# A two-layer graph network on one core: gates as diagonal products in nine blocks, another step count at the end, and gathers issued in twos

## The chip, the core and the metric

The kernel runs on one core of a Trainium2 chip. A core has five engines that work side by side, each on its own queue of instructions in order: PE (matrix products, with weight loads shown apart as PEld), DVE (vector work), ACT (activations, scaled copies), POOL (here: the indirect gathers) and SP (here: it issues the plain DMA transfers). They wait for one another through semaphores. The metric is device time in microseconds for one execution; each version is timed in several runs and the median is compared.

## What is computed

Four layers, each added onto the node values `x` (6250 nodes of 256 numbers), after a layer norm. The middle two halves matter most here:

```python
# layer 0, graph: 106250 edges sorted by dst
h = relu(concat([x[src], edge_attr]) @ W1 + b1)
agg = segment_sum(h, dst) / max(count, 1)
x = x + relu(concat([x, agg]) @ W2 + b2)
# layer 0, attention picks 2 of 4 experts by node
e = leaky_relu(a_src[src] + a_dst[dst])          # 131072 edges and own loops
agg = segment_sum(h[src] * softmax_over_dst(e))
gate = softmax(top2(mean_heads(layernorm(agg))))
x = x + sum_e gate[:, e] * (gelu(x @ W1[e] + b1[e]) @ W2[e] + b2[e])
# layer 1, graph
h = relu(x @ Wp.T + bp)
agg = sqrt(segment_sum(edge_weight * (h ** 2)[src], dst))
x = x + h @ W1.T + b1 + agg @ W2.T + b2
# layer 1, experts: a shared three-layer net and 4 small experts, 2 chosen by a gate
```

## The kernel before

Nodes lie in 49 blocks of 128, the node values stay in `x_all` on the chip. The work has four stages.

**First layer** (L1369 to L1545). Edges are handled 6 columns of 128 at a time; a group is three pairs of columns. For each pair `turn` transposes the edge features, `hidden` multiplies them (`ph`, L1091), adds the gathered source rows (L1417, DVE) and applies relu (L1422, ACT); `add_up` sums over destinations with 0/1 matrices (L1443). `load_sources` issues the six gathers of a group on POOL into a tile `yg` with three buffers; in the first groups a POOL copy into a small tile `seen` (L1386) stands in front of them.

**Attention, with the first expert layer woven in** (L1552 to L2142). The loop over `k` is called a tick here: 80 groups of 8 edge columns plus 5 ticks to finish. In a tick, `fetch` issues 8 gathers into `sg` (5 buffers), `score` and `weigh` work on earlier groups, `spread_out` and `add_up` sum into `acc`. `slot` is called four or five times a tick; it advances the experts by one step (`first` writes the hidden tile `hh` on ACT, L1607; `second` multiplies on), runs steps of `node_values`, and loads finished expert outputs.

**The seam.** When the sums of a range of blocks are done, `gates` computes their gates and `node_values` adds the gated expert outputs onto `x_all`: four multiply-adds on DVE for each block (L1952). Then come norm, transposes, the projection, and the write of `hp` to memory (L1996). The ranges end at 8, 16, 24, 32, 36, 40, 44 and 49 blocks. The gathers of the last stage read `hp_dram` and wait for all 49 writes.

**Last layer** (L2145 to L2473). 139 groups of six gathers on POOL (`hg`, six buffers, four groups ahead); `weights_of` builds weighted 0/1 matrices on DVE (L2390); `add_up` sums them on PE (L2411). Nodes are in 16 blocks of 4, 2 or 1. When a block is complete, `roots` adds the bias `b12` onto its node values (L2422) and takes the square root; `end_of2` finishes a node block, `gates2` and `experts2` are its expert layer. These are generators: `step_ends` advances all `end_of2` by a step, `advance(routes, 1)` the gates, `advance(layers, n)` the experts by n steps. In a group's turn up to group 103 it is one step of ends, one of routes and three of layers; from group 104 (`LATE`) two, two and four.

The order on each engine is not the order of the program text: the framework that builds the program lists instructions by its own estimate of when each is ready, so work of a later stage can stand on an engine in front of the end of an earlier one. The helpers `mm` (L1091), `transposed` (L1085) and `gather` (L1104) record all their instructions under one line each.

Of the kernel before, what the change touches and what calls it, by code (L numbers as in the profile page):

```python
# [841 lines left out]
def kernel(ctx: ExitStack, tc: tile.TileContext, a: dict, out: bass.AP):  # L842
# [74 lines left out]
    with ExitStack() as fast:  # L917
# [362 lines left out]
        with ExitStack() as layer:  # L1280
# [81 lines left out]
            with (  # L1362
# [9 lines left out]
                seen = wy.tile([P, 1], F32, name="seen")  # L1372
# [9 lines left out]
                def load_sources(q):  # L1382

                    if 1 <= q <= 3:
                        p, j = (q - 2, G1 - 1) if q > 1 else (0, 0)
                        GP.tensor_copy(seen, hbuf[p % 2][:, j, 0:1])  # L1386
                    w, g = groups1[q]
                    sources[q] = wk.tile([P, G1, D], F32, name="yg", bufs=3)
                    for j, (k, t) in enumerate(chunk(g)):
                        gather(sources[q][:, j, :], y_dram, src1[:, w, k, t : t + 1])  # L1390
# [16 lines left out]
                def hidden(k):  # L1407
                    q, j = pairs[k]
                    ph = psh.tile([P, 2, D], F32, name="ph")
                    e = et.pop(k)  # L1410
                    for i in range(2):
                        mm(
                            ph[:, i, :], lambda c: e[:, i, c * P : (c + 1) * P],
                            lambda c: w1b[:, c, :],
                        )
                    y = sources[q][:, j : j + 2, :]
                    V.tensor_add(y, ph, y)  # L1417
                    h = hbuf[q % 2]
                    if j == 0:

                        SC.activation(h[:, :, D:WS], ones[:, 0:G1].unsqueeze(2), AF.Copy)
                    SC.activation(h[:, j : j + 2, 0:D], y, AF.Relu)  # L1422
# [95 lines left out]
                load_sources(0)  # L1518
# [3 lines left out]
                load_sources(1)  # L1522
                for k in range(len(pairs)):
                    if k + 3 < len(pairs):
                        turn(k + 3)
                    if k + 1 < len(pairs):
                        hidden(k + 1)

                    q = k // NPC
                    if k % NPC == 0 and q:  # L1530
                        add_up(q - 1)
                    if k == len(pairs) - 1:
                        add_up(q)
                    if k % NPC == 1 and q + 2 < len(groups1):
                        load_sources(q + 2)
                    for n in list(work):
                        if next(n, work) is work:
                            work.remove(n)
                    if k % (NPC * NG) == 0 and k:
                        work.append(end_of(k // (NPC * NG) - 1))  # L1540
                    if k == len(pairs) - 1:
                        work.append(end_of(T - 1))
# [28 lines left out]
        def experts1():  # L1571
# [24 lines left out]
            def first(u, f0):  # L1596
# [9 lines left out]
                for f in (f0, f0 + 1):  # L1606
                    SC.activation(  # L1607
                        hidden[u][:, f, :n, :], ph[:, f - f0, :n, :], AF.Gelu,
                        bias=b1[:, e, f : f + 1],
                    )  # L1610

# [42 lines left out]

        layers = [experts1()]
        part = sums.tile([P, 3, T, H], BF16, name="part")
        with (
# [33 lines left out]
            def fetch(g):  # L1691
                got[g] = wk.tile([P, G, GW], F32, name="sg", bufs=5)
                for j in range(G):
                    gather(got[g][:, j, :], gat_dram, src2[:, g * G + j : g * G + j + 1])
# [250 lines left out]
            def node_values(ws):  # L1945
# [4 lines left out]
                for i, w in enumerate(ws):  # L1950
                    for e in range(X):
                        V.scalar_tensor_tensor(  # L1952
                            x_all[:, w, :], ys.pop((w, e)), gate[:, w, e : e + 1], x_all[:, w, :],
                            op0=OP.mult, op1=OP.add,
                        )
# [150 lines left out]
            for k in range(NA + 5):  # L2106
                if k < NA:
                    fetch(k)
# [5 lines left out]
                slot()  # L2114
                if now in range(NA):
                    score(now, 0)
                slot()
                if here in range(NA):
# [5 lines left out]
                slot()  # L2124
                if 0 <= before < NA:
                    add_up(before, 1)
                slot()
                if now in range(NA):
# [28 lines left out]
        with (  # L2157
# [62 lines left out]
            def end_of2(b, i, root):  # L2220
# [8 lines left out]
                V.tensor_add(x_all[:, w, :], x_all[:, w, :], pm)  # L2229
                st = wk.tile([P, 6], F32, name="ln_st")  # L2230
# [188 lines left out]
            def roots(b):  # L2419
                n = blocks[b][1]  # L2420
                at = slice(blocks[b][0], blocks[b][0] + n)
                V.tensor_add(  # L2422
                    x_all[:, at, :], x_all[:, at, :],
                    b12[:, None, :].to_broadcast([P, n, D]),
                )
# [23 lines left out]
            LATE = len(groups2) * 3 // 4  # L2449
# [6 lines left out]
            while k < len(groups2) or complete or coming or ends or routes or layers:  # L2456
# [6 lines left out]
                advance(layers, 1)  # L2463
                step_ends(k)
                if k >= LATE:
                    advance(layers, 1)
                    advance(routes, 1)
                while complete:
                    coming += roots(complete.pop(0))
                advance(routes, 1)  # L2470
                advance(layers, 2)
                if k >= LATE:
                    step_ends(k)  # L2473
# [72 lines left out]
```

## Time and profile before

| | us |
|---|---|
| runs | 3552.38, 3555.01, 3555.68 |
| median | 3555.01 |
| profiled execution | 3555.79 |
| its span, first to last instruction | 3554.0 |

Mean granted PE clock over the span: 0.911 of full speed. Where the stages lie in the profiled execution:

| from to, us | what |
|---|---|
| 0 to 132 | norms and first products, edge windows |
| 132 to 1425 | first layer |
| 1429 to 2424 | attention and first experts (first gather of sg to last sum of acc) |
| 2424 to 2468 | the seam |
| 2468 to 3506 | last layer, from the first to the last gather of hg |
| 3506 to 3554 | its tail |

How to read the views: the busy table by stretch gives for each engine how long it worked in it and how many instructions ran. A timeline line gives start, duration, engine, line of the kernel, operation, output and inputs with shapes, and in brackets the idle time in front of it and what ended it. A line of waits gives engine, line, what it waited for, then the total, the number of times and the longest.

### The profile page before, as it was taken

What the parts mean: (1) busy time and instruction counts of PE and PEld (TensorE: products, weight loads), DVE (VectorE), ACT (ScalarE), POOL (GpSimd) and SP (SyncE); (2) the same over time, 40 slices, a digit from 0 to 9 for tenths busy, and PEclk for the clock granted to TensorE, in tenths of its full rate; (3) what the DMA queues carried; (4) which work ended last, traced back from release to release, by engine and by line L of the source; (5) the groups of instructions that cost most, each with busy time, mean ns of one, the idle gap of its engine ahead of it and who ended that gap; (6) DMA issues with size and microseconds to landing.
All of it is one profiled execution on the core that took longest, in us unless ns stands there. A gap on an engine that the chain in (4) does not pass through costs nothing.

```text
span 3554.0 us, 57573 instructions
## 1 busy us (share of the span) xinstructions
PE 3338.9 (94%) x20063; PEld 2662.0 (75%) x20063; DVE 2170.1 (61%) x6210; ACT 1412.1 (40%) x2750; POOL 2252.3 (63%) x2367
## 2 busy tenths in 40 slices
PE   7999999999999999999999999997678988989898
PEld 3577777777777778888888888895456666666677
DVE  9999996444544444787758576977234444444464
ACT  4444444444444444444544454664011212211133
POOL 0376666666666664676656555662777777777773
PEclk9999999999999999999999999998567776777797
DMA  6456656656555554433434343553112222222221
GB/s 174 128 189 189 184 183 184 186 186 182 183 183 188 181 183 142 110 97 96 125 88 127 83 130 84 154 94 109 52 53 59 60 59 59 59 59 60 65 62 37
DMA packets 342928, 428.52 MB, mean 121 GB/s; under 512 B 139174, under 2 KB 246453, under 8 KB 342630
## 3 DMA queue, kind: packets, MB, share of 16 engines
q1 hardware_dynamic: 245174, 244.98, 22.1%
q0 software_dynamic: 89408, 178.08, 19.4%
q8 instruction: 162, 2.65, 0.3%
q10 hardware_dynamic: 8048, 1.68, 0.2%
q14 instruction: 136, 1.11, 0.1%
HBM read 382.05 MB, written 42.49 MB: 119 GB/s over the span
## 4 chain that ended last, share of the span: by engine, by line
PE 66%; POOL 14%; DMA 7%; issue 7%; DVE 4%; ACT 1%; SPq 0%; ACTq 0%; POOLq 0%; DVEq 0%
PE ph L1091 32%; POOL hg L1104 13%; PE py L1091 10%; PE pt L1085 7%; PE pe L1443 6%; PE po L1771 5%; DMA hg<-hp_dram,src 5%; PE pt L1091 2%; DMA rb<-low_dram 1%; PE pe L2411 1%; PE pa L1708 1%; PE pm L1091 1%; DVE junk L982 1%; DVE key L1240 0%; DVE order L1237 0%
## 5 line engine op out<-in xcount | busy, mean ns | idle before, releaser
L1104 POOL DMA_INDIRECT yg<-y_dram,src x882 | 847.0, 960 | 543.1 <-issue 226.7
L1104 POOL DMA_INDIRECT hg<-hp_dram,src x831 | 785.7, 946 | 269.2 <-issue 224.3
L1104 POOL DMA_INDIRECT sg<-gat_dram,src x640 | 614.1, 960 | 350.1 <-issue 161.5
L1091 PE MATMUL ph<-w1b,et 128*128 128x256 f32 x3528 | 835.7, 380 | 0.0
L1091 PEld LDWEIGHTS ph<-w1b,et 128*128 128x128 f32 x3528 | 637.0, 190 | 68.7
L2411 PE MATMUL pe<-eq,hg 128*128 128x96 f32 (+15 forms) x2036 | 439.9, 353 | 148.9 <-DMA hg<-hp_dram,src 120.6
L2411 PEld LDWEIGHTS pe<-eq,hg 128*128 128x128 f32 x2036 | 388.2, 260 | 251.8 <-issue 94.6
L1417 DVE TENSOR_TENSOR yg<-ph,yg 128x512 f32<-128x512 f32 x441 | 303.3, 688 | 375.3 <-PE ph L1091 370.7
L2390 DVE TENSOR_SCALAR eq<-px,dst,ew 128x96 f32<-128x96 f32 x831 | 262.0, 370 | 217.2 <-PE pe L2411 120.6
L1091 PE MATMUL ph<-b_all,w 128*128 128x256 f32 (+1 forms) x1600 | 387.1, 380 | 1.5 <-ACT hh L1607 1.4
L1091 PE MATMUL py<-w,hh 128*128 128x256 f32 x1568 | 383.1, 384 | 5.0 <-ACT hh L1607 4.5
L1086 ACT ACTIVATE et<-pt 128x512 f32<-128x512 f32 x441 | 262.2, 596 | 254.4 <-PE pt L1085 242.1
L1422 ACT ACTIVATE h<-yg 128x512 f32<-128x512 f32 x441 | 276.1, 626 | 215.4 <-DVE yg L1417 209.0
L1091 PEld LDWEIGHTS py<-w,hh 128*128 128x128 f32 x1568 | 288.7, 190 | 41.2 <-ACT hh L1607 6.6
L1091 PEld LDWEIGHTS ph<-b_all,w 128*128 128x128 f32 x1600 | 290.0, 190 | 33.7 <-ACT hh L1607 2.0
L1607 ACT ACTIVATE hh<-ph,b 128x256 f32<-128x256 f32 (+1 forms) x400 | 166.7, 467 | 285.6 <-PE ph L1091 279.7
L1085 PE MATMUL pt<-ident,ea 128*128 128x128 f32 x1764 | 272.1, 277 | 3.4 <-ACT et L1086 3.4
L1085 PEld LDWEIGHTS pt<-ident,ea 128*128 128x128 f32 x1764 | 210.2, 144 | 65.0 <-issue 40.4
L1771 PE MATMUL po<-pp,B 128*128 128x240 f32 (+10 forms) x1280 | 252.1, 337 | 2.2 <-DVE acc L1777 2.1
L1771 PEld LDWEIGHTS po<-pp,B 128*128 128x128 f32 x1280 | 215.6, 190 | 14.3 <-DVE acc L1777 2.8
L1443 PE MATMUL pe<-h,eq 128*32 128x257 f32 x3168 | 216.8, 384 | 3.7 <-ACT h L1422 1.9
L1443 PEld LDWEIGHTS pe<-h,eq 128*32 128x32 f32 x3168 | 96.2, 109 | 102.6 <-issue 35.0
(330 smaller groups left out, 4264.5 us busy)
## 6 DMA issues: line engine op xcount, KB each, us to landing
ea<-in_edge_attr_dram SPq DMA_DIRECT2D x147, 768.0 KB
y<-y SPq DMA_DIRECT2D x196, 128.0 KB
w<-in_L_ffn_W_dram SPq DMA_DIRECT2D x48, 512.0 KB
y<-ys SPq DMA_DIRECT2D x96, 256.0 KB
rb<-low_dram SPq DMA_DIRECT2D x80, 256.0 KB
yg<-y_dram,src POOLq DMA_INDIRECT x882
hg<-hp_dram,src POOLq DMA_INDIRECT x831
sg<-gat_dram,src POOLq DMA_INDIRECT x640
```

Of the source, the lines that this page charges most:

```text
L982: V.tensor_scalar(junk, flat, float(w * P), None, op0=OP.is_lt, op1=OP.add, accum_out=below[:, w : w + 1],)
L1085: TE.transpose(pt[:, c, :], src[:, c * P : (c + 1) * P], ident)
L1086: SC.activation(dst, pt.rearrange("p c k -> p (c k)"), AF.Copy)
L1091: TE.matmul(dst, lhs(c), rhs(c), start=c == 0, stop=c == n - 1)
L1104: GP.indirect_dma_start(out=dst, out_offset=None, in_=table[0:NP, :], in_offset=IndirectOffsetOnAxis(ap=idx, axis=0),)
L1417: V.tensor_add(y, ph, y)
L1422: SC.activation(h[:, j : j + 2, 0:D], y, AF.Relu)
L1443: TE.matmul(sums[w][b * Q : (b + 1) * Q, :], eq[k][:, j, at], h[:, i * NT + j, :], start=g == 0 and j == NT - 1, stop=g == last_of[b] and ...
L1607: SC.activation(hidden[u][:, f, :n, :], ph[:, f - f0, :n, :], AF.Gelu, bias=b1[:, e, f : f + 1],)
L1771: TE.matmul(po.rearrange("p b v -> p (b v)"), B[:, j, :], pp[:, j, 0:n, :].rearrange("p b v -> p (b v)"), start=half == 0 and j == 0, stop ...
L2390: V.tensor_scalar(equals[k][:, j, :], lanes[:, 0:NW], dst_of[:, t : t + 1], ew[:, t : t + 1], op0=OP.is_equal, op1=OP.mult,)
L2411: TE.matmul(sums[b][:, lo - t0 * P : hi - t0 * P], hg[:, j, :], eq[:, j, lo - n0 : hi - n0], start=False, stop=after >= (t0 + n) * P,)
```

## The change

Four edits.

1. First layer: `load_sources` takes a pair, not a group. `yg` tiles hold two columns, with nine buffers for three of six columns. For pairs 3 to 8 a POOL copy writes one element of each column of the gather's own tile from a relu output two pairs back, and the gathers follow it. In the loop, one or two pairs are issued per turn, up to six ahead.
2. Attention: `fetch` issues two gathers, and is called four times in a tick, after slots one to four. From the second group on, a POOL copy of the newest expert result (`newest`, set by `first`) into the gathers' tile stands in front of each two.
3. Seam: for blocks 40 to 48 (`LATER = T - 9`) the four multiply-adds become four scaled copies of the identity on ACT (`dg`, one buffer), four products on PE and one add on DVE.
4. Last layer: the bias `b12` is added in `end_of2`, block by block, and no longer in `roots`. A group's turn is a loop over one, two (from `LATE`) or three (from the last twelve groups, `LAST12`) rounds of: layers one step, ends, routes, and layers one more step (two before `LATE`).

```diff
-                def load_sources(q):
-
-                    if 1 <= q <= 3:
-                        p, j = (q - 2, G1 - 1) if q > 1 else (0, 0)
-                        GP.tensor_copy(seen, hbuf[p % 2][:, j, 0:1])
+                def load_sources(k, after):
+
+                    q, j = pairs[k]
                     w, g = groups1[q]
-                    sources[q] = wk.tile([P, G1, D], F32, name="yg", bufs=3)
-                    for j, (k, t) in enumerate(chunk(g)):
-                        gather(sources[q][:, j, :], y_dram, src1[:, w, k, t : t + 1])
+                    sources[k] = wk.tile([P, 2, D], F32, name="yg", bufs=3 * NPC)
+
+                    if NPC <= k < 3 * NPC:
+                        p, i = pairs[after]
+                        h = hbuf[p % 2][:, i, 0:1]
+                        GP.tensor_copy(sources[k][:, :, 0:1], h.unsqueeze(1).to_broadcast([P, 2, 1]))
+                    for i, (n, t) in enumerate(list(chunk(g))[j : j + 2]):
+                        gather(sources[k][:, i, :], y_dram, src1[:, w, n, t : t + 1])
...
+                    for _ in range(2):
+                        if loaded < min(k + 2 * NPC + 1, len(pairs)):
+                            load_sources(loaded, k + 1)
+                            loaded += 1
...
+                newest[0] = hidden[u][:, f0, 0, 0:1]
...
-            def fetch(g):
-                got[g] = wk.tile([P, G, GW], F32, name="sg", bufs=5)
-                for j in range(G):
+            def fetch(g, j0):
+
+                if j0 == 0:
+                    got[g] = wk.tile([P, G, GW], F32, name="sg", bufs=5)
+                if g > 0:
+                    GP.tensor_copy(
+                        got[g][:, j0 : j0 + 2, 0:1],
+                        newest[0].unsqueeze(1).to_broadcast([P, 2, 1]),
+                    )
+                for j in range(j0, j0 + 2):
                     gather(got[g][:, j, :], gat_dram, src2[:, g * G + j : g * G + j + 1])
...
+                    if w < LATER:
+                        for e in range(X):
+                            V.scalar_tensor_tensor(
+                                x_all[:, w, :], ys.pop((w, e)), gate[:, w, e : e + 1],
+                                x_all[:, w, :], op0=OP.mult, op1=OP.add,
+                            )
+                    else:
+
+                        dg = n6.tile([P, X, P], F32, name="dg", bufs=1)
+                        for e in range(X):
+                            SC.activation(dg[:, e, :], ident, AF.Copy, scale=gate[:, w, e : e + 1])
+                        py = psy.tile([P, 2, D], F32, name="py")[:, 0, :]
+                        mm(py, lambda e: dg[:, e, :], lambda e: ys.pop((w, e)), X)
+                        V.tensor_add(x_all[:, w, :], x_all[:, w, :], py)
...
                 V.tensor_add(x_all[:, w, :], x_all[:, w, :], pm)
+                V.tensor_add(x_all[:, w, :], x_all[:, w, :], b12)
...
             def roots(b):
                 n = blocks[b][1]
-                at = slice(blocks[b][0], blocks[b][0] + n)
-                V.tensor_add(
-                    x_all[:, at, :], x_all[:, at, :],
-                    b12[:, None, :].to_broadcast([P, n, D]),
-                )
...
-            LATE = len(groups2) * 3 // 4
+            LATE, LAST12 = len(groups2) * 3 // 4, len(groups2) - 12
...
-                advance(layers, 1)
-                step_ends(k)
-                if k >= LATE:
+                for n in range(1 + (k >= LATE) + (k >= LAST12)):
                     advance(layers, 1)
+                    step_ends(k)
                     advance(routes, 1)
-                while complete:
-                    coming += roots(complete.pop(0))
-                advance(routes, 1)
-                advance(layers, 2)
-                if k >= LATE:
-                    step_ends(k)
+                    if n == 0:
+                        while complete:
+                            coming += roots(complete.pop(0))
+                    advance(layers, 2 if k < LATE else 1)
                 k += 1
```

## The prediction

> **What bounds the kernel now.** I read the page's busy shares and clock first, then the busy time by stretch, then the waits and the instruction sequence at the seams between stages.
>
> ```profile
> PE 3338.9 (94%) x20063; PEld 2662.0 (75%) x20063; DVE 2170.1 (61%) x6210; ACT 1412.1 (40%) x2750; POOL 2252.3 (63%) x2367
> PEclk9999999999999999999999999998567776777797
> ```
>
> PE is busy 94% of the span, but with two meanings: its clock is full in the first 28 slices and about 0.7 after. The next table tells the stages apart (start:end, length, busy PE, PEld, DVE, ACT, POOL, then clock, DMA share, GB/s).
>
> ```profile
> 600.00:800.00 200.00, 200.00 (x1440) 158.68 (x1433) 90.69 (x255) 93.38 (x195) 132.68 (x139) 1.00 0.62 184
> ...
> 1440.00:2424.00 984.00, 975.51 (x6788) 867.38 (x6785) 711.17 (x1745) 499.19 (x871) 605.99 (x632) 1.00 0.41 107
> ...
> 2427.00:2464.00 37.00, 25.18 (x121) 18.56 (x119) 33.68 (x109) 22.87 (x55) 4.07 (x3) 0.91 0.58 176
> ...
> 3474.00:3495.00 21.00, 20.98 (x77) 18.62 (x77) 8.68 (x37) 4.80 (x11) 15.95 (x17) 0.50 0.23 66
> ...
> 3506.00:3544.00 38.00, 35.64 (x209) 27.49 (x207) 26.26 (x124) 23.52 (x58) 0.32 (x1) 1.00 0.06 17
> ```
>
> First layer: PE has no idle time at full clock. Attention: 8.5 us of PE idle in 984. Then a seam, 2427 to 2464, where DVE is busy 33.7 of 37 us: blocks 40 to 48 get their gated sum, norm and projection, and nothing of the next stage may gather before the last projection lands. The last stage runs from the first to the last gather of hg:
>
> ```profile
> 2467.64 0.95 POOL L1104 DMA_INDIRECT hg<-hp_dram,src  x1 [16.20 <-DMA eb<-in_L_ffn_eb_dram]
> ...
> 3505.38 0.94 POOL L1104 DMA_INDIRECT hg<-hp_dram,src  x1 [0.30 <-issue]
> ```
>
> From 2467.64 to 3506.32 is 1038.7 us for 831 gathers, 1.25 us each, 0.94 busy and 0.30 of issue, without a break: POOL's issue sets this stage and the change leaves it alone. After it PE works off a remainder until 3544 and the output leaves. So time can only be won or lost at the edges of the first two stages, in the seam, and in the tail.
>
> **The gathers in twos.** The built order of PE, ACT and DVE is the same as before, buffer names aside, up to the seam; only POOL's changes.
>
> ```profile
> L1386 POOL COPY seen<-h x3: 198/202/203, 144.3 to 163.4; 128x1 f32<-128x1 f32 x3
> ...
> POOL sg L1104 <- DVE px L1743: 128.7, 40, 6.1
> ```
>
> First layer: three copies on POOL become six. In steady state a pair waits for the buffer freed nine pairs earlier, in place of six for a group; the work is the same and PE has no idle time to give. At the start the old copies held back nothing they did not write: nine gathers ran from 132.3 to 144.3 without a stop. The new copies write into the gathers' own tiles, so the seventh gather waits for the second pair's relu, about 141.5, in place of 139.7 (2 us), and whatever is late then is the sum at DVE. PE has ph in three buffers and idled 6.5 us of 50 between 130 and 180. I take +1 us; bounds -3 (half of that idle) and +4 (two pairs' gathers late).
>
> Attention: 316 copies on POOL, four a tick, each 0.20 us by the row above; there the next gather started 1.29 us after the last instead of 1.25, so a copy mostly fits in the issue gap. At worst a tick needs 8 x 1.25 + 4 x 0.2 = 10.8 us of POOL; a tick lasts 968.4 / 79 = 12.3 us (first and last equality of rb, 1437.2 and 2405.6, 80 of them). The copy waits for the newest ACT result, and behind it wait the gathers of its tick, used three ticks (37 us) later. ACT in turn must not overwrite the hidden tile before the copy has read it; it has two buffers and comes back some four expert steps later, 9.7 us (100 units of four steps in 968.4 us). So I cost it at nothing: the 1.5 us a tick that POOL has left over hide it, and if they did not, 80 x 0.8 = 64 us would be exposed. Bounds: -5 (much of the 8.5 us of PE idle) and +6 (a few short ticks in which ACT waits on POOL).
>
> **The seam.** Nine blocks lose four multiply-adds on DVE each and get four ACT copies of the identity scaled by the gate, four matmuls and one add.
>
> ```profile
> L1952 DVE SCALAR_TENSOR_TENSOR x_all<-y,gate,x_all 128x256 f32<-128x256 f32 x196 | 86.1, 474 | 0.7 <-DMA y<-y 0.2
> ...
> L1989 ACT ACTIVATE b_all<-py,bp 128x128 f32<-128x128 f32 x49 | 17.9, 368 | 23.3 <-PE py L1091 23.0
> L1995 ACT ACTIVATE hp<-py 128x128 f32<-128x128 f32 x49 | 13.2, 275 | 25.0 <-PE py L1993 21.5 <-DMA w<-in_L_ffn_W_dram 2.8 <-DMA hp_dram<-hp 0.6
> ...
> 2456.38 1.23 DVE L2422 TENSOR_TENSOR x_all<-x_all,b 128x1024 f32<-128x1024 f32 x1
> 2457.53 0.15 DVE L1965 RECIPROCAL ln_rs<-ln_rs 128x1 f32<-128x1 f32 x1
> 2457.60 1.21 DVE L2422 TENSOR_TENSOR x_all<-x_all,b 128x1024 f32<-128x1024 f32 x1
> 2458.72 0.15 DVE L1966 SCALAR_TENSOR_TENSOR off<-ln_mv,ln_rs 128x1 f32<-128x1 f32 x1
> ```
>
> DVE: 15.8 us of multiply-adds go (36 in this stretch), 9 x 0.42 come (an add of that shape), and the two bias adds of L2422 that stand between the last block's reciprocal and offset go as well (2.4): 33.7 - 15.8 + 3.8 - 2.4 = 19.3 us. DVE is no longer the limit. ACT: 36 scaled copies, between 0.25 (the spacing of back-to-back 128x128 activations, two in 0.61) and 0.37 (L1989, which also reads a per-partition operand), 9.0 to 13.2 us; the built order has seven table loads where the trace has five, 2 x 1.28. 22.9 + 9.0 + 2.6 = 34.5 to 38.7 us. PE: a 128x256 product of four is 1.73 us at full clock, nine of them 15.6; 25.2 + 15.6 = 40.8 us. From that comes about 2 for two 128x512 fills that ran at half clock (3.99 us), and about 4 for expert matmuls (twelve 128x256 products, 24 records, 3.98 us) that the new order puts ahead of the first diagonal product: 34.8. So the stretch of 37 us is exchanged from one engine at 34 for two at 35 to 38 which must hand each block to and fro: the scaled tile has one buffer, so ACT waits for PE at each block and PE for ACT. Bounds: -4 (PE's 34.8 with little idle, and DVE's 2.4 on the last block's chain gone) and +12 (the full ACT sum, 38.7, two thirds of a microsecond of hand-over at each of nine blocks, 6, and half the clock for a quarter of the products, 4). I take +4, PE's sum plus 6 us of hand-overs.
>
> The page "ScalarE: Activation LUTs" (section "What ACT_TABLE_LOAD costs") gives a switch 2.66 us with its drain; the two extra would then be 5.3 us and the seam +7. The rows do not show the drain: the load at 3503.79 takes 1.28 and its activation starts at 3505.08.
>
> **The tail.** In both orders I count the matmuls of this path behind the last one that uses a gather: 86 before, 59 after; one whole single-node block (46) moves in front of it. Before, these take from 3513.0 to 3544.0 on a PE that is 94% busy: 31.0 / 86 = 0.36 us each, so 27 fewer are 9.7 us. Against it: the bias add becomes one more 0.42 us add in each block's chain, two blocks deep in the tail (0.8), and the chain of the last block (norm, transposes, logits) shows more as PE empties. I take -7.5, between -11 (with the 4.2 us that the last gather's matmul was behind its landing, 3508.75, partly won) and -2. For the moved 9.7 us must fit before: from 3415 to 3506 PE is busy 88.5 of 91 us at clock 0.83, so only 2.5 us are free unless the clock rises; the stretch 3474 to 3495 above, busy throughout at 0.50, is where it would have to. The other 47 bias adds (20 us over 1000, for 15 us of wide ones) lie on a DVE busy under half of the last stage; if it were full they would cost 5.
>
> The page "TensorE: Matmul & The Clock Gate" (section "Part 1: The HAM clock gate") says the clock comes back after about 3.4 us of steady work. The row speaks against it: 21 us busy without a gap at 0.50. By the rule the moved work fits and the tail gains 10; by the row it runs at half speed and the gain is nearer the small bound.
>
> **Sum.** +1 + 0 + 4 - 7.5 = -2.5 us. The profiled execution took 3555.8 us (span 3554.0 and 1.8 around it), 0.8 above the median of the three runs; I apply the sum to the median: 3552.5.
>
> **The rivals.** About 0.2%, 7.1 us, is what a measurement of this kernel can tell from no change.
> - Forecast, 0.40: the seam gives back most of what the tail wins, 3552.5, own range 3548 to 3562.
> - The seam opens, 0.35: ACT and PE overlap block by block, and the end of DVE's queue is what held the projections. Seam -4, tail -10, start and attention -2: 3539. For it: DVE at 33.7 of 37, and the bias adds in front of the last block's offset. Against it: PE's new sum.
> - The single-buffered diagonal takes DVE's place, 0.25: at each block ACT writes (1.0 to 1.5 us), PE multiplies (1.73), and the next pair's transposes wait in PE's queue behind it; seam +12, tail -3, start +1: 3565. With the tail at -3 it decides from where the hand-overs exceed 11 us in the nine blocks (34.8 + 11 - 37 = +9, and the sum above +7). For it: the buffer. Against it: the built order puts other work of ACT and PE between the four copies of a block.
> - The twos do nothing, whichever of these holds: PE has 15 us of idle time in all of both stages' 130 to 180 and 1440 to 2424, which is also the most they could win.
>
> Independent errors of about 8 (seam), 4.5 (tail), 5.5 (attention) and 3.5 (start) combine to 11 us; widened for the outer cases the range is 3535 to 3568. Faster 0.35, same 0.40, slower 0.25.
>
> **What would show it.** Seam: the first gather of hg near 2472; DVE under 25 us busy between the last gates and it, ACT or PE above 33. Tail: last gather to last matmul near 30 us, from 37.7. Attention: L1743's wait on POOL replaced by waits on hh, PE idle still under 12 us. It is wrong if PE idles more than 15 us in the attention, if the hg gathers no longer come every 1.25 us, or if the seam ends earlier than 2464.

## The result, and the profile after

| | before | after |
|---|---|---|
| median, us (runs) | 3555.35 (4) | 3577.05 (4) |
| lowest to highest | 3552.38 to 3559.82 | 3575.96 to 3579.52 |
| ratio | | 1.0061, 95% interval 1.0049 to 1.0073 |
| span of the profiled execution | 3554.0 | 3574.1 |
| granted clock of PE, mean | 0.911 | 0.919 |

The change makes the kernel 0.6% slower, about 22 us. The prediction was 3552.5 with a range of 3535 to 3568, so the time lies 9 us above the range and 12 above the slower rival.

In the runs e5 to e8 and e9 to e12 below, each set taken together, every kernel took over 4250 us, the unchanged one too (medians 4359.74 and 4357.78), for a reason that is not known, so these runs are compared only within their set.

The page of the kernel after: busy time by engine, and the granted clock in 40 slices.

```profile
PE 3332.0 (93%) x20135; PEld 2646.8 (74%) x20135; DVE 2166.2 (61%) x6216; ACT 1426.6 (40%) x2788; POOL 2316.5 (65%) x2686
PEclk9999999999999999999999999998557877877798
```

The totals hardly move: PE 7 us less, POOL 64 us more (the copies). The stretches tell more. Busy time by stretch of the kernel after (start:end, length, PE, PEld, DVE, ACT, POOL, clock, DMA share, GB/s); the second is the seam, from the gates of blocks 40 to 43 to the last square of hp:

```profile
1440.00:2424.00 984.00, 972.08 (x6759) 862.80 (x6758) 709.94 (x1736) 496.18 (x866) 672.44 (x949) 1.00 0.43 107
2430.96:2480.53 49.57, 40.97 (x195) 31.49 (x195) 18.14 (x75) 36.16 (x93) 4.07 (x3) 0.97 0.48 138
```

The first and the last gather of hg, from POOL's timeline after:

```profile
2482.93 0.95 POOL L1104 DMA_INDIRECT hg<-hp_dram,src  x1 [23.62 <-DVE ew L2228]
...
3522.88 0.95 POOL L1104 DMA_INDIRECT hg<-hp_dram,src  x1 [0.30 <-issue]
```

From such landmarks the 20.1 us between the two spans divide without a rest:

| stretch | before, us | after, us | difference | predicted |
|---|---|---|---|---|
| start to first gather of sg | 1429.44 | 1430.19 | +0.75 | +1 |
| to the last sum of acc | 995.44 | 998.74 | +3.30 | 0 |
| to the first gather of hg (seam) | 42.76 | 54.00 | +11.24 | +4 |
| to the last gather of hg | 1037.74 | 1039.95 | +2.21 | 0 |
| to the end (tail) | 48.62 | 51.22 | +2.60 | -7.5 |

Two terms are wrong by 7 and by 10 us; the experiments are about these. The other three differences are no larger than what the profiles differ by anyway. In the profiles of the experiments below that took the usual time, the first gather of sg comes at 1426.4 to 1429.8 us where edit 1 is absent, the attention takes 993.5 to 997.4 us where edit 2 is absent, and the gathers of hg take 1036.1 to 1039.1 us.

### The profile page after: what moved, and what is told of

Its sections match the earlier page's. It is cut to its first block, busy times and chain, and to the rows that moved or that the text cites. A ratio compares the mean times of both kernels' runs of the same rounds, so it can differ in the third digit from the quotient of the medians.

```text
span 3574.1 us, 58710 instructions
## 1 busy us (share of the span) xinstructions
PE 3332.0 (93%) x20135; PEld 2646.8 (74%) x20135; DVE 2166.2 (61%) x6216; ACT 1426.6 (40%) x2788; POOL 2316.5 (65%) x2686
## 4 chain that ended last, share of the span: by engine, by line
PE 67%; POOL 12%; issue 7%; DMA 6%; DVE 5%; ACT 1%; SPq 0%; ACTq 0%; POOLq 0%; DVEq 0%
PE ph L1091 32%; POOL hg L1104 11%; PE py L1091 10%; PE pt L1085 7%; PE pe L1445 6%; PE po L1787 5%; DMA hg<-hp_dram,src 3%; PE pt L1091 3%; PE pe L2443 3%; POOL sg L1104 1%; DMA rb<-low_dram 1%; PE pa L1724 1%; DVE junk L982 1%; DVE x_all L1969 0%; DVE key L1240 0%
## 5 line engine op out<-in xcount | busy, mean ns | idle before, releaser
L2443 PE MATMUL pe<-eq,hg 128*128 128x96 f32 (+15 forms) x2036 | 431.7, 347 | 167.3 <-DMA hg<-hp_dram,src 132.3
L2443 PEld LDWEIGHTS pe<-eq,hg 128*128 128x128 f32 x2036 | 372.6, 252 | 272.8 <-issue 103.8
```

Of the source, the lines that this page charges most:

```text
L2443: TE.matmul(sums[b][:, lo - t0 * P : hi - t0 * P], hg[:, j, :], eq[:, j, lo - n0 : hi - n0], start=False, stop=after >= (t0 + n) * P,)
```

## The experiments

"Seam" is the time from the last sum of acc to the first gather of hg, "root" from the last gather of hg to the last square root of a sum, "rest" from there to the last sum of x_all. They come from one profile each; ratios go against the kernel before, run in the same set.

| run | kernel | ratio (95%) | seam | root | rest |
|---|---|---|---|---|---|
| | before | | 42.8 | 7.8 | 31.7 |
| | after | 1.0061 (1.0049 to 1.0073) | 54.0 | 12.2 | 30.5 |
| e1 | edit 1 alone | 1.0002 (0.9993 to 1.0011) | 43.3 | 4.1 | 31.7 |
| e2 | edit 2 alone | 1.0007 (0.9998 to 1.0016) | 43.1 | 6.5 | 31.7 |
| e3 | edit 3 alone | 1.0051 (1.0037 to 1.0064) | 61.7 | 5.4 | 31.7 |
| e4 | edit 4 alone | 1.0012 (1.0003 to 1.0021) | 44.7 | 12.3 | 30.5 |
| e13 | after, next pair early | 1.0048 (1.0032 to 1.0065) | 52.9 | 12.3 | 30.4 |
| e14 | after, three buffers | 1.0065 (1.0048 to 1.0081) | 57.8 | 14.1 | 28.9 |
| e15 | e4, equalities earlier | 1.0032 (1.0022 to 1.0042) | 44.7 | 19.8 | 29.6 |
| e16 | e4, third step stopped | 0.9998 (0.9988 to 1.0007) | 43.7 | 9.2 | 27.2 |
| e17 | before, half the products | 1.0059 (1.0042 to 1.0076) | 52.1 | 6.0 | 42.3 |
| e18 | after without edit 3 | 1.0026 (1.0016 to 1.0035) | 42.9 | 12.3 | 30.5 |

**Each edit by itself (e1 to e4).** The lines of edit 1, 2, 3 or 4 of the diff, put alone into the kernel before.

> The kernel before with the first layer's gathers in twos and nothing else. Theory (each stage's difference between the two traces belongs to the edit in that stage): the first gather of sg starts 0.75 us later, at 1430.2 in place of 1429.4, nothing later changes, and the time is 0 to +2 us against before. Rival (the stages are coupled: a different order on POOL at the start also shifts the attention): the attention's 995.2 us from its first gather to its last sum grows by some of the 3.3 us seen with all parts, and the time is +3 to +5 us.

The first gather of sg came at 1429.01, and the attention took 994.5 us. Neither theory's cost is there: edit 1 alone does nothing that can be measured (the interval of the time is -2.5 to +3.9 us).

> The kernel before with the attention's gathers in twos behind copies, and nothing else. Theory: the stretch from the first gather of sg to the last sum is 998.5 us in place of 995.2, the seam behind it stays 43.0 us (last sum to first gather of hg), and the time is +3 to +4 us against before. Rival (the copies on POOL and the waits of ACT for them are what delays the seam): the seam grows too, by most of the 11 us seen with all parts, and the time is +10 us or more.

Attention 995.7 us and seam 43.1: the rival falls. The 3 to 4 us of the theory are not in this profile either, though the interval of the time (-0.7 to +5.7 us) does not exclude them. With all parts the attention took 998.7, 998.3 (e13) and 1002.6 (e14), with all but the diagonals 997.5 (e18). But e4, which leaves the attention as it was, took 997.4, just under the lowest of these, so whether edit 2 costs anything together with the others is not shown.

> The kernel before with the diagonal products for the last nine blocks, and nothing else. Theory (the diagonals alone open the seam): the attention stays 995.2 us, the seam from the last sum to the first gather of hg is 52 to 55 us in place of 43.0, the tail behind the last gather of hg stays 48.6 us, and the time is +9 to +12 us against before. The wide bias adds still stand in DVE's queue at the end of the seam here, so up to 2.4 us more. Rival (the seam is long only because the attention ends in another order on POOL and ACT): the seam stays within 2 us of 43 and the time within 3 us of before.

The theory's side holds, but the price is higher than it said: a seam of 61.7 us, and a time 17 us over before (medians 3571.73 and 3554.67). DVE's timeline of this kernel shows why it is worse alone than with edit 4:

```profile
2458.62 1.22 DVE L2434 TENSOR_TENSOR x_all<-x_all,b 128x1024 f32<-128x1024 f32 x1
2459.76 0.42 DVE L1969 BATCH_NORM_STATS2 ln_st<-x_all 128x6 f32<-128x256 f32 x1
2460.09 1.21 DVE L2434 TENSOR_TENSOR x_all<-x_all,b 128x1024 f32<-128x1024 f32 x1
...
2464.36 1.19 DVE L2434 TENSOR_TENSOR x_all<-x_all,b 128x1024 f32<-128x1024 f32 x1
2465.47 0.15 DVE L1971 TENSOR_SCALAR ln_rs<-ln_mv 128x1 f32<-128x1 f32 x1
```

The wide bias adds of the next stage, of which two stood in front of the last offset before, now stand one by one between the steps of a norm. PE then waited 6.46 us for that norm's xn. With all four edits the seam is 61.7 - 54.0 = 7.7 us shorter; as edits 1 and 2 leave it alone, this is put down to edit 4, which takes these adds away.

> The kernel before with three steps in the last twelve ticks and the bias added in each node block's own step, and nothing else. Theory (the extra steps stand ahead of the last gathers' products in PE's and DVE's queues, so the last block's root comes 4 us later and gives back what the shorter remainder saves): the stretch behind the last gather of hg is 50 to 52 us in place of 48.6, the seam is 2 to 3 us shorter without the wide adds in DVE's queue, and the time is 0 to +3 us against before. Rival (the tail was long with all parts only because the clock of TensorE fell to 0.59 in one stretch of 10 us): behind the last gather it is 43 us or less here, and the time is 6 to 9 us under before.

The tail is 51.7 us, as the theory had it; the rival's 43 is far off. But the seam did not get shorter without the wide adds (44.7). That is the first sign that it did not wait for these 7 us of DVE's work.

**The seam without the diagonals, and with other makers and buffers (e5 to e8).** Each changes one thing in the kernel after.

```diff
 e5  -  dg = n6.tile([P, X, P], F32, name="dg", bufs=1)
     +  dg = wk.tile([P, HG, P], F32, name="B", bufs=3)
 e6  as e5, and
     -  SC.activation(dg[:, e, :], ident, AF.Copy, scale=gate[:, w, e : e + 1])
     +  GP.tensor_scalar(dg[:, e, :], ident, gate[:, w, e : e + 1], None, op0=OP.mult)
 e7  -  if w < LATER:
     +  if w < LATER or w % 2 == 0:
 e8  -  LATER = T - 9
     +  LATER = T
```

> The changed kernel with the scaled identity in the three buffers of tile B, which the attention has done with by then, in place of one buffer of its own. The stretch from the last sum of the attention to the first gather of hg was 54.0 us in the changed kernel and 42.8 before. Theory (PE's queue makes the pairs serial: the next pair's diagonal products stand behind this pair's transposes, which wait for its norm): only the waits of PE for the scaled identity go, 1.1 us in some of the pairs, so the stretch is 50 to 53 us and the time 1 to 4 us under the changed kernel. Rival (the single buffer is what makes ACT and PE take turns, as the prediction's slower side had it): the stretch falls to 43 to 46 us and the time by 8 to 11 us, to within 0.3 to 0.4% of before.

> As the run with three buffers, and POOL, which is idle in that stretch, writes the scaled identities in place of ACT. Theory (PE's queue): ACT was not what the pairs waited for, so the stretch is within 2 us of the run with three buffers. Rival (ACT's queue is the limit: 36 scaled copies and the table loads between them, 38 us by the prediction's full sum): ACT loses 36 copies of 0.3 us, and the stretch is 6 to 10 us shorter than with three buffers.

> The changed kernel with diagonal products for the odd ones of the last nine blocks only (41, 43, 45, 47), the even ones by DVE as before. Theory (PE's queue): one product of 2.0 us in each pair's chain in place of two and DVE's sum of the other beside it, so four pairs get 1.5 to 2 us shorter each: the stretch is 46 to 49 us in place of 54.0. Rival (DVE's queue is what held the stretch before, so half of its work away must shorten it against before): under 42 us.

> The changed kernel without the diagonal products: the gathers in twos and the three steps stay. Theory (the diagonals cost the seam 10 to 12 us, and the rest of the change costs 5 to 6 in all): the stretch is 43 to 45 us and the time 3 to 7 us over before. Rival (with the steps of the tail the seam is long anyway, because the order of the queues is made anew): the stretch stays over 48 us.

Seams: 57.5 (e5), 57.3 (e6), 50.3 (e7), 43.5 (e8). POOL as maker gives nothing over ACT, though ACT is then busy for 24.2 us of the stretch in place of 36.0, so ACT's 36 copies are not the limit; and three buffers leave the seam 14 us above the one without products, over both the theory's 50 to 53 and the rival's 43 to 46. Half the products do not bring it under 42, as the rival of e7 had it. The ratios against the kernel before are 0.9824 (0.9787 to 0.9860), 0.9840 (0.9793 to 0.9888), 0.9802 (0.9765 to 0.9840) and 0.9800 (0.9763 to 0.9837). They are not taken for a gain, as no run at the usual time shows it. In these eight profiles the attention takes 1235 to 1252 us with the twos and 1312 us without (e12), so edit 2 may have won something here that it does not win otherwise; this was not followed up.

**The same again, and the bias alone (e9 to e12).** e9, e10 and e11 are e5, e7 and e8; e12 is the kernel before with `V.tensor_add(x_all[:, w, :], x_all[:, w, :], b12)` in `end_of2` in place of the wide add in `roots`.

> The same kernel as the first run with three buffers for the scaled identity, again, since in that call every kernel, the one before too, took over 4260 us. Theory (PE's queue makes the pairs serial): from the last sum of the attention to the first gather of hg 50 to 53 us (54.0 in the changed kernel, 42.8 before), and the time 1 to 4 us under the changed kernel, 3573 to 3576. Rival (the single buffer makes ACT and PE take turns): 43 to 46 us, and 3566 to 3569.

> Again, for the same reason: diagonal products for blocks 41, 43, 45 and 47 only. Theory (PE's queue): 46 to 49 us for the stretch in place of 54.0, and 3569 to 3573 us. Rival (DVE's queue is what held the stretch before, so taking half of its work must shorten it against before): under 42 us.

> Again, for the same reason: the changed kernel without the diagonal products. Theory (the diagonals cost this stretch 10 to 12 us and the rest of the change 5 to 6 in all): 43 to 45 us for the stretch, and 3558 to 3562 us. Rival (the stretch is long anyway, with the queues in a new order): over 48 us.

> The kernel before with the bias added in each node block's own step in place of the wide adds, and nothing else. Theory (the tail's loss with the three steps comes from the steps, not from the adds; DVE has time in the last stage): from the last gather of hg to the last root 4 to 8 us as before, from there to the last sum 32 to 33 us (31.7 before, and two adds of 0.42 in the chain of the last two blocks), the stretch at the seam 40 to 43 us, and the time within 2 us of before. Rival (the adds, 49 more instructions in DVE's queue, delay the equalities and so the last root): last root 12 us behind the last gather, as with the whole of that part, and the time +3 us.

Seams 58.2 (e9), 47.9 (e10), 42.9 (e11) and 45.0 (e12); ratios 0.9826 (0.9788 to 0.9863), 0.9802 (0.9763 to 0.9840), 0.9793 (0.9756 to 0.9830) and 1.0014 (0.9987 to 1.0042). The order of the seams is that of the first set. For the bias alone the interval of the time is too wide to tell its theories apart, but the profile contradicts the theory: from the last root to the last sum it took 42.2 us, not 32 to 33. PE waited 2.8 us there for the norm of the last block. As the other kernels of these sets have rests of 28.9 to 30.8 us, like those of their kind at the usual time, this is not put down to the longer runs; e17 below shows the same.

**Order and buffers, at the usual time (e13, e14).** e14 is e5. e13 adds to it that a pair of blocks frees the way for the next one after its sums, not after its norm:

```diff
                     yield w == ws[-1]
                 n = len(ws)
+                if w >= LATER:
+                    begun.remove(ws)
...
-                begun.remove(ws)
+                if w < LATER:
+                    begun.remove(ws)
```

> The changed kernel with three buffers for the scaled identity, and the next pair's products begun as soon as this pair's sums are done, so that they stand in PE's queue ahead of this pair's transposes. From the last sum of the attention to the first gather of hg it was 54.0 us in the changed kernel and 42.8 before. Theory (the order in PE's queue makes the pairs serial, not the buffer and not the amount of work): the stretch falls to 45 to 49 us, since PE's own sum for a pair is 6.8 us (two products 4.0, transposes 0.9, projection 1.2, transposes back 0.7) against 8.2 us from pair to pair in the changed kernel. Rival (the amount: ACT and PE together have more to do than DVE had): it stays over 52 us.

> Once more the changed kernel with three buffers for the scaled identity and nothing else; in two calls every kernel took over 4260 us, the one before too. Theory (order in PE's queue): 50 to 53 us for the stretch. Rival (the single buffer): 43 to 46 us.

Three buffers: 57.8, no gain at all, so the single buffer is not the cause. PE's waits in the seam show it too, first in after and then in e14:

```profile
PE py L2007 <- ACT xn L1997: 4.6, 4, 1.6
PE py L1091 <- ACT dg L1977: 2.7, 4, 1.1
```

```profile
PE py L2007 <- ACT xn L1997: 5.9, 4, 1.6
PE py L1091 <- ACT B L1977: 1.0, 1, 1.0
```

The wait for the scaled identity falls from 2.7 to 1.0 us, and the wait for the norm grows. The other order on top of the three buffers: 52.9, so the theory's 45 to 49 falls and the rival's "over 52" holds. Against e14, which differs from it by the order alone, that is 4.9 us less, but 3.0 of them are PE's own work, done at a higher clock. The seam's stretch in e13 and e14, as above:

```profile
2428.55:2475.46 46.91, 40.10 (x195) 31.85 (x195) 18.51 (x75) 34.41 (x92) 4.07 (x3) 0.96 0.44 130
```

```profile
2436.03:2488.38 52.35, 43.11 (x195) 33.55 (x195) 18.07 (x75) 36.10 (x93) 4.07 (x3) 0.93 0.37 109
```

PE alone has 40 us of work, more than the whole stretch of 37.0 took before.

**The tail (e15, e16).**

```diff
 e15  -  name="eq", bufs=3          +  name="eq", bufs=5
      -  weights_of(k + 1)          +  weights_of(k + 3)
 e16  -  for n in range(1 + (k >= LATE) + (k >= LAST12)):
      +  for n in range(1 + (k >= LATE) + (k >= LAST12 and not 0 < len(groups2) - k <= 4)):
```

In e15 the equalities of the first three groups are made ahead of the loop.

> The kernel before with the three steps and the bias per block, and with the equalities of each group of gathers made three groups ahead in place of one (five buffers in place of three). With the three steps alone the last root came 12.3 us behind the last gather of hg (4 to 8 in runs without them), and from there to the last sum it was 30.4 us (31.7 without). Theory A (the last group's equalities wait in DVE's queue behind the extra steps, which wait for PE and ACT): with the equalities ready, the last root comes 6 to 9 us behind the last gather, and the time is 3 to 6 us under that of the three steps alone. Theory B (the extra steps' products themselves stand in PE's queue ahead of the last group's, so the work was moved ahead of a product that it delays): 10 to 12 us, and the time within 2 us of the three steps alone.

> The kernel before with the three steps and the bias per block, but without the third step in the last four ticks of the gathers. Theory (the sum of work on PE behind the last gather is what sets the end, and the steps only exchange work before the last root for work behind it): the last root 6 to 9 us behind the last gather, and 32 to 34 us from there to the last sum, together 39 to 42 as before (39.5) and under the 42.7 with the three steps everywhere. Rival (the eight ticks before that had filled PE already): the last root still 11 us or more behind the last gather.

With the equalities ready the last root comes later still, 19.8 us behind the last gather. The stretch between the two in e15:

```profile
3508.00:3528.00 20.00, 20.00 (x119) 15.72 (x117) 12.76 (x57) 10.93 (x28) 0.95 (x1) 1.00 0.08 21
```

PE works without a gap: the last group's six products stand at 3526.99 in its queue, behind the steps. Theory A falls; theory B is right about the place and too low in size, and why the root comes even later than in e4 was not found. In e16 the last root comes 9.2 us behind the last gather, about as its theory had it. The rest is shorter than it said, 27.2 us, and the two together are 36.3, under its 39 to 42: the sum is not just exchanged. The time is that of before.

**Half the products (e17), and no products (e18).** e17 is the kernel before with the bias per block, the three buffers and the early pair, and `if w < LATER or w % 2 == 0:`; e18 is e8.

> The kernel before with the bias per block, diagonal products for blocks 41, 43, 45 and 47 only, in the three buffers of tile B, and the next pair begun as soon as the sums of this one are done. It is to tell whether a smaller share of products beats DVE's sums. Busy time in the stretch from the gates of blocks 40 to 43 to the last square of hp: before PE 25 and DVE 34 of 37 us, of which 6 us of DVE are wide bias adds; here PE about 32, DVE about 21, ACT about 29. Theory (no engine's sum but the chain of each pair bounds it, and each product lengthens that chain): 38 to 43 us, the time 0 to +4 us against before. Rival (DVE's queue bounded it): 31 to 35 us, the time -3 to -6 us.

> The changed kernel without the diagonal products, once more. Theory (the terms of the four parts add up, with the diagonals at 11 us and more when alone): the last sum of the attention to the first gather of hg 43 to 45 us, and the time +4 to +8 us against before. Rival: over 48 us for the stretch.

e18 is within 0.2 us of what its theory had, and its median (3563.42 against 3555.18, +8.2) leaves about 13 us of the change's 22 to edit 3. e17 is worse than its theory said, and its rival falls. The stretch of the seam in e18 and in e17:

```profile
2430.60:2467.59 36.99, 25.36 (x121) 18.60 (x119) 26.59 (x102) 24.28 (x57) 4.07 (x3) 0.91 0.59 177
```

```profile
2422.32:2469.06 46.74, 34.87 (x155) 25.96 (x155) 23.09 (x90) 31.60 (x74) 4.07 (x3) 0.89 0.47 141
```

In e18 DVE has 7 us less to do than before and the stretch is the same 37 us. In e17 no engine is over 35 of 46.7 us. PE's timeline there shows one of its gaps; the product of block 47, whose scaled identity was ready 7 us earlier, stands in the queue behind transposes that wait for the norm of the pair before:

```profile
2452.99 0.44 PE L1997 MATMUL py<-ident,xn 128*128 128x128 f32 x2 [2.93 <-ACT xn L1986]
2453.27 3.31 PE L1091 MATMUL py<-y,B 128*128 128x256 f32 x8
```

## Why the prediction was wrong

**The bound of the seam was misread.** "A seam, 2427 to 2464, where DVE is busy 33.7 of 37 us" was taken for "exchanged from one engine at 34". Busy is not bounding: about 7 of those 34 us are wide bias adds for the next stage, of which the sum took off only 2.4, and without them (e4, e18) the stretch stays at 38.7 and 37.0. Most of them stand in one row of DVE's timeline before:

```profile
2458.79 8.03 DVE L2422 TENSOR_TENSOR x_all<-x_all,b 128x1024 f32<-128x1024 f32 x7
```

The view that would have told it was at hand, the chain of waits of the kernel before in this window. Some of its pieces (start, us, what):

```profile
2424.63 0.92 PE py L1091 x4
2425.55 0.86 PE ph L1091 x4
2426.41 1.73 PE py L1091 x8
2428.14 2.63 PE ph L1091 x16
...
2437.70 1.74 PE py L1091 x8
2439.44 0.02 issue
2439.46 0.70 DVE ys L1623
...
2447.30 3.55 POOL g L2203 x2
2450.86 0.05 issue
2450.90 0.54 POOL nothing L2218
2451.44 0.04 issue
2451.49 2.08 PE pe L2406 x2
```

One DVE piece is in it, 0.70 us, and it is not a gated sum. The chain runs over PE and ACT and three fills on POOL (two of g, one of nothing). The change took work from an engine that was not on this chain and put it on one that was. That does not make DVE idle or far from it: its last step before that piece, and the same place in the chain of e18, are

```profile
2439.23 0.16 DVE L1966 SCALAR_TENSOR_TENSOR off<-ln_mv,ln_rs 128x2 f32<-128x2 f32 x1
```

```profile
2443.02 0.16 DVE off L1991
2443.18 0.67 DVE ys L1629
```

Before, DVE was ready at 2439.39 and PE's product at 2439.44; in e18 the chain runs over DVE from 2428.4 to 2443.9, and its stretch is the same 37 us. So in the first half of the seam the queues of DVE and of PE with ACT were level, and in the second half PE waited 4.66 us for the fills on POOL:

```profile
2451.49 2.08 PE L2406 MATMUL pe<-nothing,ident 128*128 128x512 f32 x2 [4.66 <-POOL nothing L2218]
```

What is shown is that the seam does not get shorter by unloading DVE at PE's expense; what unloading DVE's gated sums alone would do, no run shows.

**The step that failed in the seam: PE's sum was trimmed to 34.8, and it was 40.97.** "25.2 + 15.6 = 40.8" was trimmed by 2 us for fills at half clock and by 4 for expert products that "the new order puts ahead". The first was right: the fills took 2.05 us after, 3.99 before. The second was not: the expert products stayed in the stretch, 56 records and 11.5 us after, 54 and 10.7 before. And the nine diagonal products took 17.9 us, 2.0 each in place of 1.73. So it is partly luck that the untrimmed sum meets the measured one. ACT (34.5 to 38.7 predicted, 36.2 measured) and DVE (19.3 predicted, 18.1 measured) came near. Hand-overs were put at 6 us; PE idled 49.57 - 40.97 = 8.6. The stretch thus grew by 15.8 us of PE's work, less 3.2 us of idle time (11.8 before): +12.6, where the prediction had 34.8 + 6 - 37 = +4. The seam came out at +11.2.

**The slower rival had the price and not the cause.** It put +12 on the single buffer. Three buffers won nothing (e14), and another maker nothing (e6 against e5). What is left is PE's queue. Its amount, 41 us with nine products, is alone longer than the old stretch of 37.0, so about 4 of the 12.6 us could not be won back by better overlap of the work that stands there. The rest is waiting in turn, as one pair of blocks in the chain of after shows, 9.1 us from its transposes to those of the next:

```profile
2462.73 0.44 PE py L2007 x2
2463.17 1.99 PE py L1091 x8
2465.20 0.04 issue
2465.24 0.40 ACT dg L1977
...
2470.70 1.08 ACT xn L1997 x2
2471.82 0.44 PE py L2007 x2
```

How much of it is the order of the queue was not settled: e13's new order is worth 1.1 us against after and 4.9 against e14, and e17's fewer products left 12 us of idle PE, of which the gap of 2.9 us shown above comes from the order.

**The tail.** The count was right: 86 to 59 matmuls behind the last one that uses a gather. In the window behind the last root, two records to a matmul, before and after:

```profile
3513.20:3544.87 31.67, 29.02 (x168) 22.01 (x167) 21.04 (x105) 20.44 (x51) 0.00 (x0) 1.00 0.05 17
```

```profile
3535.11:3565.57 30.46, 24.16 (x114) 18.19 (x114) 16.09 (x78) 14.28 (x36) 0.00 (x0) 0.80 0.03 9
```

168 less 114 is 54, or 27 matmuls. The step that failed is "27 fewer are 9.7 us", by which the tail was to gain 7.5 us; it lost 2.6. There are three reasons. First, the count was made from the last gather's own product, and that product is not fixed in time: the moved steps stand ahead of it, and the last root came 12.2 us behind the last gather in place of 7.8 (4.1 to 7.8 in all kernels at the usual time without the third step). In after, PE stood 1.71 us for the last equalities, which DVE could not make before it had done with the moved steps; e15 shows that making them early only shows PE's queue as the next limit. Second, with less to do PE runs empty, and then its clock falls: 114 records would take 29.02 x 114 / 168 = 19.7 us at the rate of before, and took 24.2. PE's idle time grew from 2.7 to 6.3 us. So 9.3 us of work less became 1.2 us of time, and 4.4 us were lost ahead of it. e16 is the counterpart: with 120 records, its clock 0.93 and its PE time 21.7 us, its rest is 27.2. Third, the bias add was put at 0.8 us. Both kernels that have it without the third step (e12 and e17) have a rest of 42.2 and 42.3 us with as many matmuls as before and one more, some 10.5 us longer: PE waits 2.8 us for the norm of the last block, 0.8 before, and then runs at a lower clock (0.84 and 0.81). Counted from there, the third step shortens the rest by 11.8 us, more than the 9.7 predicted, and delays the root by some 6. So the bias add may be the larger part of the error; at the usual time it was not run by itself.

**The twos.** First layer +0.75 us, +1 predicted; alone nothing, and profiles differ by more, so the agreement is luck. Attention +3.3 for 0, inside its bounds (-5 to +6), and PE idles 11.9 of 984 us, under the 12 given. The copies do wait for ACT as said, in place of the wait on px; from the waits on POOL after, 1440 to 2424:

```profile
POOL sg L1104 <- issue: 132.7, 422, 2.1
...
POOL sg L1705 <- ACT hh L1612: 113.1, 56, 6.5
```

**The gathers of hg** took 2.2 us more, 1.253 us each for 1.250. No edit is seen to cause it: e18, with edits 1, 2 and 4, took 1037.98 us, and e13, with all four, 1037.37.

The range failed because two errors had the same sign. It combined the seam and the tail as independent; both come in part from giving PE's queue more to do ahead of something that waits. Of the signs that were to tell, DVE under 25 us and ACT or PE above 33 came true (18.1, 36.2 and 41.0) with the seam at nearly three times its price: they fit a slow seam as well as a fast one. The first gather of hg near 2472 did not (2482.93).

## What to carry to other kernels

Read what bounds a short stretch from the chain of waits in that window, not from the engine with the highest busy share: work of a later stage may fill an engine without anything waiting for it. Then ask which other queue is about as long, since the chain names only one of them. Work moved "ahead of the end" in an in-order queue is ahead of something else too; ask what product, and whether the end starts from it. Where nothing beat the kernel before, the nearest was e16, the third step stopped four groups early; the three fills on POOL in the chain above, 4.1 us, would be the next place to look, which was not tried.

## What the hardware showed that was not expected

PE's clock falls after quite short idle times and stays low for longer than they last. Busy time by stretch in the tail after:

```profile
3530.00:3532.00 2.00, 2.00 (x10) 1.20 (x9) 1.03 (x7) 1.34 (x4) 0.00 (x0) 1.00 0.00 0
3532.00:3536.00 4.00, 1.36 (x8) 0.87 (x6) 3.42 (x15) 2.78 (x5) 0.00 (x0) 1.00 0.00 0
3536.00:3540.00 4.00, 2.76 (x9) 2.12 (x10) 1.62 (x5) 0.98 (x2) 0.00 (x0) 0.50 0.10 33
3540.00:3546.00 6.00, 6.00 (x25) 5.64 (x26) 2.77 (x15) 2.54 (x5) 0.00 (x0) 0.50 0.00 0
3546.00:3548.00 2.00, 1.70 (x9) 1.00 (x8) 0.59 (x4) 1.82 (x4) 0.00 (x0) 0.93 0.00 0
```

In 3532 to 3536 PE was busy 1.36 of 4 us, with no single gap above 1.71. Then it runs at half clock until after 3546, of which 6 us without a pause. The tails of before, e1 and e2 have no such gap, and their rest is 31.7 us each time. In e17 PE idled 2.77 us at 3532.1, worked again from 3534.9 without a pause, and ran at half clock to about 3549.3; that is some 6 to 7 of the 10.6 us by which its rest is longer. The row in which its clock comes back, and two of its products, in the low and in the full clock:

```profile
3548.00:3550.00 2.00, 2.00 (x11) 1.72 (x10) 1.31 (x7) 0.68 (x2) 0.00 (x0) 0.68 0.00 0
```

```profile
3537.41 1.20 PE L1091 MATMUL py<-sw,h 128*128 128x256 f32 x2
...
3550.47 0.70 PE L1091 MATMUL py<-sw,h 128*128 128x256 f32 x2
```

The Trainium skill's page "TensorE: Matmul & The Clock Gate", section "Part 1: The HAM clock gate (the "warmup" mystery)", gives about 3.4 us for both: idle for one such window halves the clock, and one busy window restores it. Here two gaps of 1.7 and 1.0 us with 1.0 us of work between were enough, and it took 6 us of steady work and more in after, and 14 us in e17 (3534.9 to 3549.3), until it was restored.
